# Linear attention: where a unit's score matmuls stand in TensorE's hand-written order

## Chip, cores, metric

One core of a Trainium2 chip runs the whole program in one launch. The metric is the device time of that launch in microseconds; 14 runs of the kernel before gave a median of 2377.67 us, from 2363.53 to 2383.84.

## What is computed

The program is a stack of four layers on `x` of shape (4, 1024, 128) in float32. Each layer is an attention-like part and a feed-forward part, each with a residual and a layer norm. Only the third layer's attention and feed-forward part, and how they interleave, matter here. The attention is a causal linear attention with 16 heads of 64, written in the reference as a scan over time:

```python
Qp, Kp = relu(x @ Wq + bq), relu(x @ Wk + bk)      # V = x @ Wv + bv
Qc, Qs = Qp * cos(a_t), Qp * sin(a_t)              # a_t = pi * t / (2 T)
Kc, Ks = Kp * cos(a_t), Kp * sin(a_t)
S_cos += Kc_t V_t^T ; S_sin += Ks_t V_t^T ; z_cos += Kc_t ; z_sin += Ks_t
out_t = (Qc_t S_cos + Qs_t S_sin) / max(Qc_t z_cos + Qs_t z_sin, 1e-6)
y = out @ Wo + bo
```

The feed-forward part is a mixture of 8 experts: a softmax router picks two per row, and each row's result is the weighted sum of two gated MLPs (128 to 2 x 256 to 128).

## The kernel before, in words

**Units.** The attention (`l2_attn`, L920) cuts the time axis of each of the four sequences into four quarters of 256 rows, and each quarter into eight pairs of heads: 128 units. In a unit the 256 rows are two chunks (c) of 128. Within a chunk the kernel uses the product form: scores of all keys with all queries, multiplied by a fixed matrix (`c_near`: the cosine of the distance, zero above the diagonal). What lies before a chunk comes from running sums of keys with values, carried from chunk to chunk.

**The steps of a unit.** The letters in the list are only for reading:

- `l2_project` (L1045): TensorE makes the queries and keys of the unit (tile pqk, a bank called pj); ScalarE applies relu and writes r_q and r_k; GpSimd multiplies r_q with the cosines and sines (qt).
- `l2_keys` (L1065): two TensorE transposes of r_k into the bank kp; ScalarE writes them out four times scaled (kN). In the last quarter of a sequence only one chunk's keys are needed.
- `l2_scores` (L1106): eight matmuls, 16 instructions in the trace since each float32 matmul takes two passes, of 64 rows by 64 columns, into the banks pa0 and pa1. VectorE multiplies each of the two with `c_near` and writes the tile a (L1119), which holds the scores for the next step.
- `l2_before` (L1138): queries qt with the carried sums st, into the bank po.
- `l2_within` (L1154): a with the values cv, on top of it in po.
- `l2_sums` (L1082): kN with the values, 128 rows by 64 columns, into the bank kp (pst); VectorE adds the carried sums and writes the new ones, st (L1098 to L1103; one or two instructions).
- `l2_out` (L1164): VectorE divides: dn (L1171), a reciprocal, co (L1173).

**The order on TensorE.** TensorE's order in this stage is the order in which the loop at L966 issues; `manual_schedule` at L965 says so. Iteration t holds work of three units: keys of unit t+1, projection of unit t+2, scores of t+1, then before and within of unit t, the sums of t+1, and l2_out of t. All other engines have an order made by a scheduler. Between the sums and the next iteration's key transposes stands extra work that only some iterations have: values of the next quarter (pv, VectorE evacuates them as cv), output transposes (pt, ScalarE copies them as coT), output projections (pr), the normalisation of four chunks and its transposes, the router and the dispatch of the experts. A list `side` of generators advances one step per iteration.

**The expert tiles.** Once a sequence's rows are dispatched, `early(moe)` at L988 advances the mixture of experts by one tile of 128 rows per iteration: every fourth time the transposes of four row tiles (pt<-xg), then the hidden matmuls of one tile (`l2_hidden`, L1474: eight instructions), then the output of the tile two before (`l2_expert_out`, L1498: py, four instructions). ScalarE and VectorE make tanh, sg and mh out of the hidden matmuls; ScalarE copies py to ys.

**Shared banks.** Three PSUM banks are shared by slices, which is written in three lines:

```python
for t in (("pa0", "m0"), ("pa1", "m1"), ("kp", "mo")):
    v = two.tile([P, 512], F32, name="_".join(t))
    self.psq.update({t[0]: (v, 0), t[1]: (v, 3 * P if t[0] == "kp" else 2 * P)})
```

So pa0 takes the left half of a bank for the scores and m0 the right half for the experts' hidden matmuls; likewise pa1 and m1; and kp holds key transposes and pst on the left, and mo, the expert output py, on the right. There is one buffer of each. The trace calls these tiles pa_m and kp_mo.

Of the kernel before, what the change touches and what calls it, by code (L numbers as in the profile page):

```python
# [58 lines left out]
class Net:  # L59
# [42 lines left out]
    def load(self, name, shape, pool=None, tag=None, eng=None):  # L102
        pool = pool or self.const
        t = pool.tile(shape, F32, name=f"sb_{name}", tag=tag or f"sb_{name}")
        src = self.io[name]
        (eng or self.nc.sync).dma_start(out=t, in_=src)
        return t
# [812 lines left out]
    def l2_attn(self, load, dispatch, moe, first):  # L920

        nc, tc = self.nc, self.tc
        NQ = 2
        with ExitStack() as ctx:
            wp = ctx.enter_context(tc.tile_pool(name="cos", bufs=2))
            self.c2["wp"] = wp  # L930
            quarters = [
                dict(b=b, q=q, c0=q * NQ, x=self.xT[b][:, q * NQ * P : (q + 1) * NQ * P])
                for b in range(B)
                for q in range(NC // NQ)
            ]
            units = [dict(Q=Q, hp=hp) for Q in quarters for hp in range(NP2)]
            self.psq = {}
            for t, n in dict(pj=2, po=1).items():
                self.psq[t] = ctx.enter_context(
                    tc.tile_pool(name=f"ps_{t}", bufs=n, space=bass.MemoryType.PSUM)  # L940
                )

            two = ctx.enter_context(
                tc.tile_pool(name="ps_two", bufs=1, space=bass.MemoryType.PSUM)
# [4 lines that stand above are left out]
            v = two.tile([P, 512], F32, name="pr_sx")  # L949
            self.psq.update(pr=(v, 0), sx=(v, 2 * P))  # L950
            self.mtags = dict(t="pj", h=("m0", "m1"), o="mo")
            self.l2_tiles(quarters[0], None)
            for f in self.l2_values(quarters[0]):
                pass
            n = len(units)
            side, begin = [], None

            def early(moe):

                if "done" not in self.m2["st"][1]:  # L960
                    for k in range(1):
                        next(moe)


            ctx.enter_context(tc.manual_schedule(engines={mybir.EngineType.PE}))  # L965
            for t in range(-2, n + 4):  # L966
                if t == 0:
                    load()
                if 0 <= t + 1 < n:
                    u = units[t + 1]  # L970
                    if u["hp"] == 0:
                        i = (t + 1) // NP2
                        if i + 1 < len(quarters):
                            nxt = quarters[i + 1]
                            self.l2_tiles(nxt, quarters[i])
                            side.append(self.l2_values(nxt))
                    self.l2_keys(u)
                if 0 <= t + 2 < n:
                    self.l2_project(units[t + 2])
                if 0 <= t + 1 < n:  # L980
                    self.l2_scores(units[t + 1])
                if 0 <= t < n:
                    self.l2_before(units[t])
                    self.l2_within(units[t])
                if 0 <= t + 1 < n:
                    self.l2_sums(units[t + 1])
                if "put" in self.m2["st"][0] if t > 0 else False:
                    early(moe)  # L988
                    if "done" in self.m2["st"][0]:

                        if begin is None:
                            begin = self.l3_prepare(self.l3_early(first))
                        next(begin, None)
                if 0 <= t < n:
                    self.l2_out(units[t])
                    if t % 4 == 3:
                        Q = units[t]["Q"]
                        g = self.l2_project_out(Q, t % NP2 // 4)
                        if t % NP2 == NP2 - 1 and Q["c0"] + NQ == NC:
                            g = chain(g, dispatch(Q["b"]))  # L1000
                        side.append(g)
                for g in side[:]:
                    if next(g, self) is self:
                        side.remove(g)
            for g in (begin, *side):
                for f in g:
                    if f == "put":
                        self.m2["rest"] = g
                        break
# [1193 lines left out]
```

## Time and profile before

| what | number |
|---|---|
| median of 14 runs | 2377.67 us (2363.53 to 2383.84) |
| the profiled execution | 2381.47 us, span 2379.7 us |
| granted TensorE clock, mean over the span | 0.907 |
| first and last score multiplication a (L1119) | 643.3 and 1369.3 us |
| hidden matmuls of experts in the attention's banks | 360 instructions, 988.7 to 1384.6 us |

The attention is the stretch from about 641 to 1375 us. After it follows the last layer, a state-space layer and another mixture of experts, with the remaining expert tiles in between.

In the views, PE is TensorE, PEld its weight loads, DVE VectorE, ACT ScalarE, POOL GpSimd. A row of the timeline gives start, duration, engine, line, operation, output tile <- input tiles and shape; in square brackets stands the engine's idle time before it and what ended it. Neighbouring instructions of one kind are merged into one row (x16), so a matmul row's start is the start of its group and its duration ends with the last, modelled, end. Matmuls overlap: the time a group costs is read from its start to the start of the next group. A row of the waits reads "engine, tile, line <- engine, tile, line that ended the wait: us in total, times, longest". A row of the table of stages gives the stretch, its length, then busy time and instruction count of PE, PEld, DVE, ACT and POOL, the granted clock, the DMA share and GB/s.

### The profile page before, as it was taken

The page shows a single profiled execution, that of the slowest core. Times are in us where ns is not written, and L with a number is a line of the kernel's source. Part 1 is how long each engine was busy: PE and PEld are TensorE (multiplying, and loading weights), DVE is VectorE, ACT ScalarE, POOL GpSimd, SP SyncE. Part 2 cuts the span into 40 slices and gives each one's busy share as a digit, 9 for nine tenths or more (in the row PEclk, how much of TensorE's full clock was granted, in tenths as well). Part 3 has the DMA queues.
Part 4 walks back from the last instruction along what each step waited for, and adds up shares of the span by engine and source line. Part 5 has one row for each costly group of instructions (what it writes and reads, how often), then busy time and mean ns, then how long its engine had stood idle before and what let it go on. Part 6 is the DMA issues. An engine that isn't in the chain of part 4 may idle for free. (4 is left out here: it accounts for less than half of the span.)

```text
span 2379.7 us, 46470 instructions
## 1 busy us (share of the span) xinstructions
PE 2035.2 (86%) x17858; PEld 1425.4 (60%) x17858; DVE 1349.5 (57%) x3661; ACT 1206.0 (51%) x2619; POOL 1025.3 (43%) x813
## 2 busy tenths in 40 slices
PE   6667979879999999999979856778898989799988
PEld 3455655444477777787767654345565556465666
DVE  6457733433355554654545536776767777676421
ACT  6543433332244444454446536565758776667443
POOL 5001220000123234134143328988887998678400
PEclk9757969979999999999989978979999999899999
DMA  3000110005000010021222046555775766575411
GB/s 103 0 18 18 31 35 1 18 13 164 1 3 3 2 36 23 24 86 36 78 70 82 16 157 189 165 161 173 207 208 140 202 172 178 165 196 157 118 58 49
DMA packets 138702, 211.63 MB, mean 89 GB/s; under 512 B 18613, under 2 KB 75952, under 8 KB 138096
## 3 DMA queue, kind: packets, MB, share of 16 engines
q1 hardware_dynamic: 126192, 173.87, 23.8%
q0 software_dynamic: 12288, 34.79, 6.9%
q8 instruction: 141, 2.31, 0.4%
q14 instruction: 81, 0.66, 0.1%
HBM read 160.29 MB, written 23.16 MB: 77 GB/s over the span
## 5 line engine op out<-in xcount | busy, mean ns | idle before, releaser
L1061 POOL TENSOR_TENSOR qt<-r_q,sb_c_turn 128x256 f32<-128x256 f32 (+1 forms) x256 | 164.3, 663 | 460.7 <-ACT r_q L1053 455.1
L1861 POOL TENSOR_TENSOR hc<-db,cn 128x1024 f32<-128x1024 f32 x128 | 311.7, 2460 | 72.9 <-PE pys L127 24.4
L1845 POOL TENSOR_TENSOR db<-ud,bn 128x1024 f32<-128x1024 f32 x112 | 283.7, 2590 | 32.6 <-DVE ud L1809 16.8
L127 PEld LDWEIGHTS py<-wh,hh 128*128 128x128 f32 x2048 | 253.8, 197 | 72.8 <-issue 37.0
L127 PE MATMUL ph<-xT,wh 128*128 128x512 f32 x512 | 264.1, 633 | 24.1 <-ACT hh L1973 5.2
L127 PE MATMUL py<-wh,hh 128*128 128x128 f32 x2048 | 260.0, 281 | 17.5 <-ACT hh L1973 14.1
L1973 ACT ACTIVATE hh<-ph,sb_cols 128x512 f32<-128x512 f32 x256 | 171.8, 682 | 136.3 <-PE ph L127 109.5
L1119 DVE TENSOR_TENSOR a<-pa_m,sb_c_near 128x256 f32<-128x256 f32 x256 | 96.5, 419 | 215.1 <-PE pa_m L127 215.1
L1076 ACT ACTIVATE kN<-kp_mo,sb_c_trig 128x128 f32<-128x128 f32 x448 | 130.1, 372 | 132.1 <-PE kp_mo L131 119.3
L1849 ACT ACTIVATE da<-dl,aneg 128x512 f32<-128x512 f32 x224 | 153.4, 689 | 75.6 <-DVE db L1850 67.8
L127 PE MATMUL pys<-hc,sb_c_ident 128*128 128x512 f32 x320 | 163.0, 635 | 9.8 <-DMA hc<-hc 6.4
L1850 DVE TENSOR_TENSOR_SCAN db<-da,carry,db 128x512 f32<-128x512 f32 x128 | 157.2, 1266 | 11.7 <-ACT da L1849 7.0
L127 PEld LDWEIGHTS ph<-xT,wh 128*128 128x128 f32 x512 | 91.6, 200 | 114.4 <-issue 56.0
L1850 DVE TENSOR_TENSOR_SCAN db<-da,db 128x512 f32<-128x512 f32 x128 | 149.7, 1206 | 8.9 <-ACT da L1849 5.7
L1989 DVE SCALAR_TENSOR_TENSOR h_acc<-py,gt,h_acc 128x128 f32<-128x128 f32 x256 | 71.6, 342 | 138.2 <-PE py L127 138.2
L127 PE MATMUL pqk<-xT,wE 128*128 128x256 f32 x512 | 139.5, 396 | 7.9 <-ACT coT L1195 4.2
L729 POOL DMA_INDIRECT orows<-o,ix x20 | 18.9, 945 | 203.3 <-DVE o L727 169.1
L127 PEld LDWEIGHTS pys<-hc,sb_c_ident 128*128 128x128 f32 x320 | 61.6, 205 | 73.3 <-issue 59.0
L127 PEld LDWEIGHTS pqk<-xT,wE 128*128 128x128 f32 x512 | 90.6, 197 | 22.4 <-DVE cv L1038 8.1
L1195 ACT COPY coT<-pt 128x512 f32<-128x512 f32 x64 | 37.5, 586 | 125.5 <-PE pt L131 125.5
L131 PE MATMUL pt<-sb_c_ident,xN 128*128 128x128 f32 x224 | 54.1, 344 | 51.9 <-ACT xN L174 33.9
L127 PE MATMUL po<-ht,wD 128*128 128x512 f32 x192 | 93.7, 595 | 0.0
(450 smaller groups left out, 4403.8 us busy)
## 6 DMA issues: line engine op xcount, KB each, us to landing
wx<-in_wF SPq DMA_DIRECT2D x92, 384.0 KB
bn<-rows SPq DMA_DIRECT2D x128, 256.0 KB
cn<-rows SPq DMA_DIRECT2D x128, 256.0 KB
wh<-in_wH SPq DMA_DIRECT2D x64, 512.0 KB
hc<-hc POOLq DMA_DIRECT2D x48, 512.0 KB
xrows<-zero SPq DMA_DIRECT2D x4, 1472.0 KB
xg<-xrows SPq DMA_DIRECT2D x20, 256.0 KB
yrows<-ys SPq DMA_DIRECT2D x20, 256.0 KB
```

The lines of the kernel that those rows point to most:

```text
L127: return self.nc.tensor.matmul(out=out, lhsT=lhsT, rhs=rhs, start=start, stop=stop)
L131: self.nc.tensor.transpose(out, in_, self.ident[0:n, 0:n])
L1061: nc.gpsimd.tensor_mul(u["qt"][:, m, a:], u["q"][:, a:], c2["turn"][:, m, o + a : o + 2 * P])
L1076: self.nc.scalar.activation(u["kN"][:, c, m, :], pk[:, c, :], AF.Copy, scale=trig[:, k, m : m + 1])
L1119: nc.vector.tensor_mul(u["a"][:, i, :, :], pa[i], self.c2["near"][:, None, :].to_broadcast([P, 2, P]),)
L1195: nc.scalar.copy(oT, pt)
L1845: nc.gpsimd.tensor_mul(db, ud, bc[0])
L1849: nc.scalar.activation(da, dl[:, ec, :], AF.Exp, scale=aneg[:, j : j + 1])
L1850: nc.vector.tensor_tensor_scan(db[:, ec, :], da, db[:, ec, :], carry[:, ec, n : n + 1] if h else 0.0, ALU.mult, ALU.add,)
L1861: nc.gpsimd.tensor_mul(hc, db, bc[1])
L1973: nc.scalar.activation(ht, ph, AF.Relu, bias=self.col("h_b1", i=e * NK + k))
L1989: nc.vector.scalar_tensor_tensor(acc[:, c, :], py[:, c, :], gt[:, c, e : e + 1], acc[:, c, :], ALU.mult, ALU.add,)
```

## The change

The scores of unit t+1 are issued behind the sums of unit t+1 and no longer behind the projection of unit t+2. In an iteration TensorE's order was keys, projection, scores, before, within, sums; it is now keys, projection, before, within, sums, scores, and then the expert tile and the side work as they were. Scores of a unit are still made one iteration ahead of the within step that uses them.

```diff
                     self.l2_keys(u)
                 if 0 <= t + 2 < n:
                     self.l2_project(units[t + 2])
-                if 0 <= t + 1 < n:
-                    self.l2_scores(units[t + 1])
                 if 0 <= t < n:
                     self.l2_before(units[t])
                     self.l2_within(units[t])
                 if 0 <= t + 1 < n:
                     self.l2_sums(units[t + 1])
+                    self.l2_scores(units[t + 1])
                 if "put" in self.m2["st"][0] if t > 0 else False:
                     early(moe)
```

## The prediction

> **What bounds the kernel now.** I read the page's first two parts, then the table of stages (busy time of each engine in three stretches of the linear attention), then TensorE's waits in those stretches, then the timeline of single units. The profiled execution took 2381.47 us around a span of 2379.7; the median of the 14 runs is 2377.67, so what I work out in this trace is added to the median.
>
> ```profile
> span 2379.7 us, 46470 instructions
> PE 2035.2 (86%) x17858; PEld 1425.4 (60%) x17858; DVE 1349.5 (57%) x3661; ACT 1206.0 (51%) x2619; POOL 1025.3 (43%) x813
> ```
>
> ```profile
> 640.00:985.00 345.00, 323.21 (x6037) 259.03 (x6035) 185.98 (x623) 149.71 (x437) 110.95 (x182) 0.98 0.04 12
> 985.00:1305.00 320.00, 291.67 (x4668) 243.67 (x4668) 173.63 (x637) 157.19 (x466) 104.55 (x150) 0.95 0.23 68
> 1305.00:1375.00 70.00, 59.14 (x1049) 47.78 (x1047) 38.40 (x116) 37.38 (x85) 22.07 (x28) 0.93 0.11 31
> ```
>
> In each row the second number is the length and the third TensorE's (PE's) busy time: 94%, 91% and 84%. The attention runs from 641 to 1375 us and TensorE bounds it; VectorE (DVE) is about half busy. What TensorE waits for there is short:
>
> ```profile
> PE kp_mo L131 <- DVE st L1103: 14.6, 14, 2.7
> PE kp_mo L127 <- DVE st L1103: 10.1, 5, 2.2
> ```
>
> Both rows are one kind of wait: the bank that is named kp in its left columns and mo in its right columns is written again only after VectorE has read the key-value sums (pst) out of it. In the first row the next unit's key transposes wait, in the second the expert output py. That one writes the mo columns, which the sums never touch, and waits all the same.
>
> A unit with no extra work, whose end shows the first wait:
>
> ```profile
> 710.15 0.67 PE L127 MATMUL pa_m<-r_q,r_k 64*64 64x128 f32 x16
> ...
> 710.63 0.65 PE L1128 MATMUL po<-st,qt 64*64 64x65 f32 x32
> ...
> 711.21 0.69 PE L1128 MATMUL po<-cv,a 128*64 128x65 f32 x16
> ...
> 711.73 0.64 PE L127 MATMUL kp_mo<-cv,kN 128*64 128x65 f32 x16
> ...
> 712.69 0.28 DVE L1100 TENSOR_TENSOR st<-kp_mo,st 128x130 f32<-128x130 f32 x1
> 713.01 0.29 DVE L1103 TENSOR_TENSOR st<-kp_mo,st 128x130 f32<-128x130 f32 x1
> ...
> 713.45 0.41 PE L131 MATMUL kp_mo<-sb_c_ident,r_k 128*128 128x128 f32 x2 [1.08 <-DVE st L1103]
> ```
>
> Read the starts: scores 710.15, before 710.63, within 711.21, sums 711.73; VectorE ends its second st at 713.30 and the transposes start 0.15 later, 2.24 after within. VectorE needs that long because dn, the reciprocal, co and two st stand one behind another once within is done. And a unit that also carries an expert tile:
>
> ```profile
> 1037.53 0.69 PE L1128 MATMUL po<-cv,a 128*64 128x65 f32 x16
> ...
> 1038.62 1.16 PE L127 MATMUL pa_m<-xgT,wx 128*128 128x128 f32 x8
> ...
> 1039.33 0.29 DVE L1103 TENSOR_TENSOR st<-kp_mo,st 128x130 f32<-128x130 f32 x1
> ...
> 1039.68 0.71 PE L127 MATMUL kp_mo<-wx,mh 128*128 128x128 f32 x4
> ```
>
> The expert's hidden matmuls start right behind the sums, 1.09 after within, and write the m0 and m1 columns of the two banks whose pa0 and pa1 columns take the scores.
>
> **The change, part by part.** No instruction is added or removed; 16 score matmuls of each of 128 units move, and with them the two multiplications a. No DMA and no GpSimd work moves.
>
> *(1) The scores leave their place before before.* They take 0.48 us there (710.15 to 710.63). So within, the sums, and VectorE's dn to st come 0.48 earlier after the transposes. The keys kN must then be ready 0.48 earlier for the sums: in most units ScalarE ends the last kN 0.7 to 1.9 us ahead of the sums, so this costs nothing. (In one unit with little slack, at 1283, up to 0.4 would show.)
>
> *(2) The scores come behind the sums.* They cost 0.48 again, and one change of array shape more than before. Today a unit changes from 128x128 to 64x64 (into the scores), to 128x64 (into within) and back to 128x128: three. Afterwards: into before, into within, into the scores, and back: four. Price of one from the rows: before's 32 instructions run at 0.058 per four, which is 0.46, but within starts 0.58 after them, 0.11 more; the projection's four run at 0.215 each and the scores start 0.10 later than that pace. I take 0.10. Bounds: nothing, as from within to the sums, which share a shape, and 0.15. The Trainium skill, "TensorEngine Tiling (Array Packing)", Key Properties, says that a change of tiling mode drains the engine, which speaks against the new place and agrees with these spacings; without such a cost the 73 units of (3) that pay it would keep 7 us.
>
> *(3) The wait of the transposes shrinks.* The moved scores, about 0.59 with their changes of shape, lie in it. Where the wait is longer than that, a unit gains the whole 0.48; where there is none it loses 0.10; in between it loses 0.10 less the wait. Over the 88 units without an expert tile, from the start of each unit's groups: 11 with 0.6 to 1.16 us of wait (the unit without extra work; a first output transpose that waits for co) gain 0.48, in sum -5.3; 12 with waits of 0.19 to 0.59 give -3.2; 8 with 0.16 behind pr give -0.4; four, where a normalisation or the state-space work on VectorE or ScalarE ends last, give 0, since that chain starts from r_q and r_k and not from the scores; the other 53 lose 0.10, +5.3. Sum: **-3.6 us**.
>
> *(4) The multiplication a is now fresh when the expert's matmuls come.* In the built program's order VectorE has dn, reciprocal, co, st, st, a, a in every unit. The expert's first hidden matmul waits for an a on pa0 and its third for the a on pa1, in both programs; but so far these were a of scores issued two groups of matmuls earlier, long done, and now they are the a of the scores just in front. The price: st ends at within + 2.09 (1039.62 - 1037.53); an a takes 0.415 and two in a row 0.75, so one behind st adds 0.34; the release takes 0.15 as above. The hidden matmuls start at within + 2.58 in place of 1.09: 1.49 later, and with (1)'s 0.48 back, **+1.01 per unit**. The second a ends 0.34 after the first, while the first four hidden matmuls take 0.45, so it adds nothing. Behind them stand the expert output, values, output projection and the next transposes on TensorE, all of which shift; tanh, sg and mh shift too, but their tile is used two units later. (2)'s switch and the scores themselves vanish in this wait.
>
> The page has 45 tiles' hidden matmuls (360 instructions, eight each); 5 come after the last scores, 40 inside. 21 plain ones: 21 x 1.01 = 21.2. Ten have row transposes xg ahead (hidden at within + 1.58 today): 1.00 less 0.48, 5.2. Four are in a last quarter with one st: there a waits for the scores instead (they end about within + 1.5), +0.8 each, 3.2. Five are units with a normalisation, where py waits for a late st today; afterwards the hidden matmuls start 0.49 behind that st (0.34 and 0.15) and py 0.89 later (eight at the 0.11 that four in 0.45 make), where it was 0.15: 1.23 each, 6.2; the 0.48 isn't regained, since the chain to that st starts from r_q and r_k. Sum: **+35.8 us**.
>
> The Trainium skill, "PSUM — Partial Sum Buffer", section on bank collisions, tells authors to guard by bank and quadrant, not by address; by that rule the wait in (4) is needed, while by addresses (4) would fall away, these units would lose about 0.10 each, and the total would be near zero. The row of py that waits for st is the trace's own case of the former.
>
> *After the attention* the order on ScalarE and VectorE differs in places (two table loads of 1.28 fewer on ScalarE). I cost it at 0, within 5 us either way. The state-space stage follows on the same engines, so the delay passes on.
>
> **Sum:** -3.6 + 35.8 = +32, so 2381.5 + 32 = 2413.5 in the terms of the profiled run, **2410 us** against the median.
>
> **The rivals.**
>
> *The wait (4) is not exposed* (6%): if both a were done by the time the hidden matmuls are reached, about 1.7 after within, they would start at once. Nothing in VectorE's own speed speaks for it: a stands behind st in the order, and st alone ends at within + 2.09. Then the 40 units lose 0.10 each, +4.0, and the sum is 2378: no change.
>
> *Shape changes cost nothing and the wait shrinks* (6%): with (4) not exposed and a switch price of 0 in place of 0.10, the 113 units that pay it (53, 12 and 8 without an expert tile, the 40 with one) keep 11.3, and 2367 is left: faster, by over 0.3% once a switch costs under 0.04. The spacing from within to the sums speaks for it, the other two and part (4) against.
>
> *The new waits also lower the clock or meet a second bound* (15%): TensorE would stand idle some 1 us in each of 40 units; the table's granted clock falls from 0.98 to 0.95 already where idle is greatest. If the expert stretch fell to 0.92, its 292 busy us would grow by about 9: 2420. Against it: between 645 and 750 waits of 1.1 us recur and the clock stands at 1.00.
>
> *Waits partly taken back* (8%): where the transposes today wait 0.52 for the copy of py, or where DMA or a normalisation ends last, a shift of 1.01 may overlap; half of (4): 2392.
>
> **How the numbers follow.** The forecast, 65%, 2400 to 2420 by (2)'s bounds and the 5 us of the tail. Range with the neighbours 2390 to 2424. A measurement of this kernel can tell about 0.3%, 7 us, from no change. Faster 6%, within 0.3% 6%, slower 88%.
>
> **What would show it.** TensorE's waits must show hidden matmuls (pa_m<-xgT,wx) held by DVE a for 0.7 to 1.1 us some 40 times; transposes held by st much less (14.6 us to about 8); units without extra work 4.0 us apart and not 4.5; units with plain expert tile 6.8 where they were 5.8. If hidden matmuls do not wait, (4) is wrong and with it the sign; if the spacing from the sums to the scores is 0.05, (2) is.

## The result, and the profile after

The changed kernel takes **2403.6 us** (median of 13 runs, 2396.1 to 2415.7), the kernel before 2377.05 in the same comparison (62 runs): a ratio of 1.0117 [1.0102, 1.0132], 26.6 us more. The forecast was 2410, within 2390 to 2424.

The profiled execution was shorter than the 13 timed ones (2394.0 us around its span); a second profile of the same program has a span of 2414.7. The page of the first:

```profile
span 2392.2 us, 46443 instructions
...
PE 2029.8 (85%) x17858; PEld 1415.7 (59%) x17858; DVE 1336.4 (56%) x3661; ACT 1201.8 (50%) x2617; POOL 1023.5 (43%) x813
```

TensorE does the same 17858 instructions in no more busy time (2029.8 us for 2035.2); what is new is time between them. The table of stages, with borders shifted so that each stretch holds the same work as the row of before:

```profile
635.00:980.00 345.00, 329.68 (x6036) 258.09 (x6035) 179.64 (x623) 149.05 (x437) 110.41 (x182) 0.99 0.04 12
980.00:1328.00 348.00, 299.54 (x4667) 243.75 (x4666) 168.80 (x636) 157.86 (x466) 104.14 (x150) 0.95 0.22 62
1328.00:1395.00 67.00, 56.76 (x1051) 44.86 (x1049) 38.01 (x117) 36.92 (x86) 22.02 (x28) 1.00 0.11 33
```

The first stretch, without expert tiles, is as long as before (345). The second, which has nearly all of them, grew from 320 to 348 at the same granted clock of 0.95. The third lost 3. So the loss is in the stretch with the expert tiles, and on the mean it isn't the clock. What TensorE waits for between 640 and 1405 us:

```profile
PE pa_m L127 <- DVE a L1118: 35.2, 33, 3.5
...
PE kp_mo L131 <- DVE st L1102: 7.3, 11, 1.5
```

The first row is new: matmuls that write the pa/m banks, held by the multiplication a (L1118 is L1119 of before). The second is the wait that the change shortens: it had 14.6 us. The row of py held by st (10.1 us) is gone. Who waits for a, from the view of that line:

```profile
who waited for it (us, times):
  PEld pa_m L127: 45.8, 40
  PE pa_m L127: 35.2, 33
  ACT L1489: 9.1, 4
```

Weight loads in front of hidden matmuls wait 40 times, as many as there are expert tiles inside the attention. A unit without extra work, in the timeline:

```profile
704.85 0.70 PE L1127 MATMUL po<-st,qt 64*64 64x65 f32 x32
...
705.48 0.69 PE L1127 MATMUL po<-cv,a 128*64 128x65 f32 x16
...
706.00 0.64 PE L127 MATMUL kp_mo<-cv,kN 128*64 128x65 f32 x16
...
706.56 0.67 PE L127 MATMUL pa_m<-r_q,r_k 64*64 64x128 f32 x16
...
707.28 0.29 DVE L1102 TENSOR_TENSOR st<-kp_mo,st 128x130 f32<-128x130 f32 x1
...
707.72 0.41 PE L131 MATMUL kp_mo<-sb_c_ident,r_k 128*128 128x128 f32 x2 [0.49 <-DVE st L1102]
```

The scores (706.56) lie where TensorE stood idle. The transposes still start 2.24 after within, but within comes 0.46 earlier, and the unit takes 4.05 us in place of 4.51. That is the gain. A plain unit with an expert tile shows the price:

```profile
1037.94 0.69 PE L1127 MATMUL po<-cv,a 128*64 128x65 f32 x16
...
1038.45 0.64 PE L127 MATMUL kp_mo<-cv,kN 128*64 128x65 f32 x16
...
1039.02 0.67 PE L127 MATMUL pa_m<-r_q,r_k 64*64 64x128 f32 x16
...
1039.73 0.29 DVE L1102 TENSOR_TENSOR st<-kp_mo,st 128x130 f32<-128x130 f32 x1
1039.94 0.74 DVE L1118 TENSOR_TENSOR a<-pa_m,sb_c_near 128x256 f32<-128x256 f32 x2
1040.04 0.98 POOL L1382 DMA_INDIRECT xrows<-xN,di  x1 [0.16 <-issue]
1040.41 0.30 PEld L127 LDWEIGHTS pa_m<-xgT,wx 128*128 128x128 f32 x2 [0.97 <-DVE a L1118]
1040.41 0.38 PE L127 MATMUL pa_m<-xgT,wx 128*128 128x128 f32 x1 [0.73 <-DVE a L1118]
```

The scores are issued by 1039.6, and then TensorE stands until VectorE, which has dn, the reciprocal, co and two st ahead of it, is through with the first a. The hidden matmuls start 2.47 after within, where it was 1.09.

### The profile page after: what moved, and what is told of

The parts are those of the page before. It is cut to its first block, busy times and chain, and to the rows that moved or that the text cites. A ratio compares the mean times of both kernels' runs of the same rounds, so it can differ in the third digit from the quotient of the medians.

```text
span 2392.2 us, 46443 instructions
## 1 busy us (share of the span) xinstructions
PE 2029.8 (85%) x17858; PEld 1415.7 (59%) x17858; DVE 1336.4 (56%) x3661; ACT 1201.8 (50%) x2617; POOL 1023.5 (43%) x813
## 4 chain that ended last, share of the span: by engine, by line
PE 41%; DVE 14%; ACT 11%; issue 4%; DMA 2%; POOL 1%; SPq 0%; DVEq 0%; ACTq 0%; POOLq 0%
PE py L127 7%; PE ph L127 7%; PE po L1127 6%; DVE db L1849 5%; PE pqk L127 4%; PE pa_m L127 4%; PE pr_sx L1197 3%; PE pys L127 2%; PE pv L127 2%; PE kp_mo L127 2%; ACT da L1848 1%; PE pt L131 1%; ACT hh L1972 1%; DMA wx<-in_wF 1%; PE kp_mo L131 1%
## 5 line engine op out<-in xcount | busy, mean ns | idle before, releaser
L1860 POOL TENSOR_TENSOR hc<-db,cn 128x1024 f32<-128x1024 f32 x128 | 329.7, 2605 | 57.3 <-DVE db L1849 19.6
L1844 POOL TENSOR_TENSOR db<-ud,bn 128x1024 f32<-128x1024 f32 x112 | 300.3, 2726 | 36.4 <-DVE ud L1808 22.6
L127 PE MATMUL ph<-xT,wh 128*128 128x512 f32 x512 | 254.2, 615 | 22.4 <-ACT hh L1972 7.2
L1170 DVE TENSOR_SCALAR dn<-po 128x4 f32<-128x4 f32 x128 | 20.5, 160 | 252.4 <-PE po L1127 252.3
L1118 DVE TENSOR_TENSOR a<-pa_m,sb_c_near 128x256 f32<-128x256 f32 x256 | 95.3, 414 | 0.5 <-PE pa_m L127 0.5
```

What stands on the lines that cost most here:

```text
L127: return self.nc.tensor.matmul(out=out, lhsT=lhsT, rhs=rhs, start=start, stop=stop)
L1118: nc.vector.tensor_mul(u["a"][:, i, :, :], pa[i], self.c2["near"][:, None, :].to_broadcast([P, 2, P]),)
L1844: nc.gpsimd.tensor_mul(db, ud, bc[0])
L1860: nc.gpsimd.tensor_mul(hc, db, bc[1])
```

## The experiments

The theory: the loss is the wait of the hidden matmuls for the fresh a, and it exists because their results share banks with the scores. The rivals: the late place costs by itself (array shapes, later values and projections), or the time behind the attention changes. "Attention" is, in each profile, the time from the first key transposes to the last co; "behind" is from there to the end.

| kernel | ratio to before [interval] | attention, us | behind, us |
|---|---|---|---|
| before (two profiles) | 1 | 732.6, 732.5 | 1005.8, 1002.7 |
| changed (two) | 1.0117 [1.0102, 1.0132] | 757.5, 763.2 | 998.5, 1012.8 |
| late_where_no_tile (two) | 1.0023 [1.0007, 1.0040] | 727.6, 728.3 | 1013.0, 1009.9 |
| late_where_tile | 1.0124 [1.0100, 1.0148] | 763.5 | 1007.9 |
| after_hidden_pj (two) | 0.9990 [0.9975, 1.0004]; 0.9986 [0.9969, 1.0003] | 724.8, 725.9 | 1015.9, 1015.8 |
| before_hidden_pj | 0.9993 [0.9972, 1.0013] | 734.4 | 1004.4 |
| scores_behind_side | 1.0060 [1.0039, 1.0081] | 748.2 | 1000.3 |
| late_where_it_pays | 0.9936 [0.9915, 0.9957] | 715.0 | 1016.4 |

**The new place only in units without, or only in units with, an expert tile.** TILES are the 40 iterations that carry a tile; the second kernel has the two conditions swapped.

```diff
+TILES = {*range(69, 84), *range(93, 116), *range(125, 127)}
...
+                tile = t in TILES
+                if 0 <= t + 1 < n and tile:
+                    self.l2_scores(units[t + 1])
                 if 0 <= t < n:
                     self.l2_before(units[t])
...
                     self.l2_sums(units[t + 1])
+                if 0 <= t + 1 < n and not (tile):
                     self.l2_scores(units[t + 1])
```

> Scores behind the sums in the 88 iterations without an expert tile, in the old place in the 40 with one. Theory (the cost is the hidden matmuls' wait for the fresh a; without a tile the move only shortens the transposes' wait): 4 to 8 us faster than before, 2370 to 2374 us, and no row of hidden matmuls waiting for a. Rival (the late place itself costs, by its extra change of array shape or by an altered order on the other engines): 5 us slower than before or more.

> The other half alone: scores behind the sums only in the 40 iterations with an expert tile. Theory: all of the loss and a little more than it, 28 to 36 us over before, some 2405 to 2413; each plain tile unit about 0.8 us longer. Rival (the late place itself costs): about a third of the loss, +9 us, since 40 of 128 units have it.

With the new place only beside tiles: 2405.6, 28 us over before; the whole loss, as expected. Without them: 2382.9, 5.6 us over before, where 4 to 8 less were expected: a miss. Its attention did get 4 to 5 us shorter. What was lost lies behind it: 1013.0 and 1009.9 us in place of 1005.8 and 1002.7. That stretch, which the edit doesn't touch, was to change by no more than 5 us in the prediction; what goes along with it is told below, under the second profiles.

**The hidden sums in a bank of their own.** They go to a buffer of pj, which the projections and the output transposes use, in the changed kernel and in the one before.

```diff
-            self.mtags = dict(t="pj", h=("m0", "m1"), o="mo")
+            self.mtags = dict(t="pj", h=("pj",), o="mo")
```

> The changed kernel with the experts' hidden matmuls in one of the two pj banks, so that they share no bank with the scores; their four matmuls then share one bank, and tanh, sg and mh are one instruction each over both halves. Theory: hidden matmuls start 0.2 us behind the scores, no wait for a, and this kernel is within 7 us of its partner with the old order of scores (before_hidden_pj). Rival (the loss is not the shared bank): still 20 us or more over its partner.

> The kernel before with the hidden matmuls in a pj bank: the partner of the run above. Both theories: within 10 us of the kernel before either way; a pj bank is busier, but tanh, sg and mh are fewer instructions. It only sets the level to compare with.

This decides it. With the order of the change left as it is, the loss is gone: 2375.0 and, in a second comparison, 2379.9 beside 2381.2. In the kernel before the same edit moves nothing that could be measured. The same unit as above, in the timeline of after_hidden_pj (the hidden sums are called ph here):

```profile
1036.92 0.69 PE L1127 MATMUL po<-cv,a 128*64 128x65 f32 x16
...
1038.01 0.67 PE L127 MATMUL pa_m<-r_q,r_k 64*64 64x128 f32 x16
...
1038.61 1.16 PE L127 MATMUL ph<-xgT,wx 128*128 128x128 f32 x8
1038.73 0.29 DVE L1102 TENSOR_TENSOR st<-kp_mo,st 128x130 f32<-128x130 f32 x1
...
1038.94 0.75 DVE L1118 TENSOR_TENSOR a<-pa_m,sb_c_near 128x256 f32<-128x256 f32 x2
```

The hidden matmuls start right behind the scores, 1.69 after within, and a runs beside them. In this kernel's view of the line of a, the list of those who waited for it is empty.

**The scores at the very end of a unit.** Behind the expert tile and the side work.

```diff
                     self.l2_sums(units[t + 1])
-                    self.l2_scores(units[t + 1])
                 if "put" in self.m2["st"][0] if t > 0 else False:
                     early(moe)
...
                     if next(g, self) is self:
                         side.remove(g)
+                if 0 <= t + 1 < n:
+                    self.l2_scores(units[t + 1])
```

> The scores of the next unit come at the very end of a unit in TensorE's order: behind the sums, the expert's tile and the other extra work. By the theory (the loss is the hidden matmuls that wait for the multiplications a of the scores just in front of them) the hidden matmuls then start right behind the sums again, about 1.1 us after within, and no hidden matmul waits for a. The other way round the scores now wait for the readers of the hidden sums, about 0 to 0.5 us in the units where the expert output is the last extra work. Expected: 2374 to 2388 us, no more than 0.5% from the kernel before. By the rival (the loss comes from the late place itself: shape changes, or key transposes and the next unit's values that come late) it stays at 2395 us or above, as in the changed kernel.

2391.3 beside 2375.1: 0.6% where at most 0.5% (2388) was expected, a miss, and 4 us below the rival's 2395. The mechanism held: hidden matmuls start 0.567 behind the start of the sums, as in the kernel before. TensorE's waits have the other way round, and little of it, and no row with a:

```profile
PE pa_m L127 <- DVE mh L1494: 1.6, 4, 0.4
```

What remains is not that wait. The stretches with tiles are 3.1 and 2.7 us longer than in before (11.0 and 16.9 in the changed kernel), but the first stretch, which has none, is 8.7 longer. In most units the scores now stand between groups of 128 by 128 on both sides, with one more change of array shape than in the changed kernel, and most units grow step by step: with values and projection 5.18 in before, 5.34 in the changed kernel, 5.49 here; with projection and transposes 4.78, 4.94, 5.07. This isn't all of it: units with values, projection and transposes are up to 0.25 shorter than in before, and no run took the shape change away alone.

**The new place where it pays.** Hidden sums in pj, and the scores early in 63 iterations (EARLY) in which, between before_hidden_pj and after_hidden_pj, the late place had made a unit 0.10 to 0.55 us longer.

```diff
-            self.mtags = dict(t="pj", h=("m0", "m1"), o="mo")
+            self.mtags = dict(t="pj", h=("pj",), o="mo")
...
+                early_t = t in EARLY
+                if 0 <= t + 1 < n and early_t:
+                    self.l2_scores(units[t + 1])
...
-                    self.l2_scores(units[t + 1])
+                if 0 <= t + 1 < n and not early_t:
+                    self.l2_scores(units[t + 1])
```

> The hidden sums in their own bank, and the new place of the scores only in the 64 iterations in which it shortened a unit by more than the added change of array shape costs or left it equal; in the 63 others (mostly units with values or an output projection behind the sums, each 0.16 us longer in the late place) the scores stay ahead of before. By the theory each of those 63 units gets its 0.16 us or more back, 63 units with 11.3 us in the two profiles with the hidden sums moved: the attention, 724.8 us from the first key transposes to the last co with the scores late everywhere and 732.6 in the kernel before, should take 714 to 718 us. The whole: 2375 less 7 to 11 is 2364 to 2368, a ratio of 0.995 to 0.997. By the rival (the gains hang on the neighbouring units and on the order that VectorE and ScalarE are given, and what the attention gains is lost behind it) 2372 or more.

> The changed kernel with the hidden sums in their own bank, once more. Attention from the first key transposes to the last co 724.8 us as in the first profile, within 1 us. The stretch behind the last co was 1015.9 us, the longest of all profiles: if it varies from execution to execution it comes out several us away, if it belongs to the program within 2 us. Time 2371 to 2378.

2367.2 beside 2381.2: 14 us faster than before, a little more than expected, and the attention took 715.0 us, within the 714 to 718 named. It beats both kernels. Beside after_hidden_pj, run on the same chip, it is 12.8 us faster. The stretch behind the attention stayed at 1016.4 in the one profile, an execution of 2375.5 us, 8 above the median.

**Second profiles, for the time behind the attention.**

> The kernel with the new place only where a unit carries no expert tile, once more for a second profile. Its attention was 5 us shorter than before's and the stretch behind the attention 7 us longer. If that stretch differs from execution to execution, it should come out different here by several us from 1013.0 us (last co to the end); if the program itself makes it longer, within about 2 us of 1013.0.

> The kernel before, a second profile: the stretch behind the last co took 1005.8 us in the first. If it varies from execution to execution, it comes out several us away; if it belongs to the program, within about 2 us.

> The changed kernel, a second profile: the attention should be the same within 1 us (last co at about 1393.8 us, hidden matmuls held by a as before); the stretch behind the last co took 998.5 us in the first. Since the first profiled execution was 9.6 us under the median of the timed ones, I expect a longer stretch here, about 1003 to 1012 us, if the spread lies behind the attention.

The attention repeats within 1.1 us for each of these programs except the changed kernel, where it differs by 5.7: jumps of 0.5 to 2.1 in four units where a run of expert tiles begins or ends. At these places the second profile's granted clock is 0.5 for 3.4 or 6.8 us longer than the first's.

Behind the attention, two profiles of a program are 0.1 to 3.1 us apart, and 14 in the changed kernel. From program to program the stretch goes from 998.5 to 1016.4. late_where_it_pays and after_hidden_pj have the same order of instructions on all engines there, and the same 1016; before_hidden_pj has another order and 1004. But late_where_tile has the changed kernel's order, and these three profiles spread from 998.5 to 1012.8, so the order doesn't settle it. The granted clock goes along with the time: in this stretch it is 0.92 in before, before_hidden_pj, late_where_tile and the changed kernel (998.5 to 1012.8 us), 0.91 in late_where_no_tile (1013.0, 1009.9) and 0.90 in after_hidden_pj and late_where_it_pays (1015.8 to 1016.4). TensorE is busy there for 843.1 and 839.4 us in before and for 853.6 to 856.7 in the last two, with as many instructions. scores_behind_side (1000.3 us at 0.91) does not fit. No run held the order or the clock alone: whether the order sets the clock, or something else does, stays open.

## Why the prediction was right

**The sign and its cause, step (4).** Held: 40 waits for a were forecast and 40 found, and taking the shared bank away takes the loss away. VectorE's order, which the prediction gives as the same in every unit, is dn, reciprocal, co, st, st, a, a in 87 of the 128; in the others an st stands ahead of co. That these sums share only a bank with the scores, and no column, is what the Trainium skill's "PSUM — Partial Sum Buffer" tells authors to guard (bank collisions); the program has that wait, and no run here shows what would happen without it.

**Its size.** A plain unit with a tile was forecast to lose 1.01 and lost **0.79** (5.46 to 6.24, 5.83 to 6.62, 6.69 to 7.48). The terms, from medians of group starts: the hidden matmuls came 0.10 earlier than costed, at within + 2.48, since the release took 0.05 (in the unit shown the first a ends at 1040.36) and not 0.15; before grew by 0.05 (a shape change at its entry); and hidden and output groups are 0.17 shorter, which the prediction had not seen: in the kernel before py waited for st in every such unit, and behind a it no longer does. 1.01 - 0.10 + 0.05 - 0.17 = 0.79. Units with row transposes lost 0.57 (0.52 forecast), last-quarter units 0.76 (0.8). Of the five units with a normalisation (1.23 forecast) iterations 82, 98, 112 and 114 lost 2.25, 2.97, 1.96 and 2.53, and 106 came out 1.19 shorter; some neighbours gave part of it back. In those four TensorE waited 2.4 to 3.2 us for a, and next to the start of the hidden matmuls the granted clock went to 0.5 for 3.4 us, so that they took 1.35 to 1.87 us up to py and not 1.00; in the kernel before this comes in one of the four, at the end of iteration 82. In late_where_tile, with the same late scores, iterations 82 and 114 have no such stretch and lost 0.64 and 0.88. So part of what they lost is the clock, which the prediction had only in a rival. All stretches with tiles, up to the last co: +11.0, +16.9 and +1.2, together **+29.1** in the first profile and +34.8 in the second, for a forecast of +35.8.

**The change of array shape, step (2).** Costed at 0.10 with 0.15 as the upper bound; measured **0.16**, outside it. From group start to group start the scores take 0.597 behind the sums, where they took 0.488, and before takes 0.626 (32 instructions) where it took 0.575. The prediction counted one change more and took the price of one. But two spacings grew, the way out of the scores into 128 by 128 by 0.11 and the way into before by 0.05.

**The shorter wait, step (3).** Units without extra work came out at 4.05 (4.0 forecast), the wait for st at 7.3 us (about 8). The sum of units without tiles is -4.3, for -3.6; but that is two misses that cancel. In the 79 units ahead of the state-space work 17 units gained 8.0, 43 lost 0.16 each, 6.9 in all, and the other 19 lost 1.4: +0.3. The last stretch, costed at nothing, gave -4.6, 3.6 of it in one unit. There VectorE had dn, the reciprocal and co between three multiplications of the state-space layer, and TensorE's output transposes waited 3.5 us for co; in the changed kernel co stands ahead of them.

**The rivals.** "Not exposed" and "shape changes cost nothing" fall by the 40 waits and the 0.16. The clock did not fall as a whole: 0.95 before and after in the stretch with tiles, and 0.92 in both behind the attention (the table of before has its lowest clock, 0.93, in the third row, where TensorE is least busy, and not 0.95 as the prediction reads it). It fell in single units, the four above. "Waits partly taken back" is what happened to py, 0.17 of the 1.01, and not to half of it.

**The sum.** Attention +24.9 and +30.7 in the two profiles, +27.8 on the mean, and behind it 1005.7 on the mean for 1004.3: together +29, for +32 forecast and +26.6 measured. That the stretch behind comes out near the 0 it was costed at is luck: the two profiles, 998.5 and 1012.8, lie on either side, further off than the 5 us allowed. The two profiles of the changed kernel differ by 22.5 us in span; 14.3 of it lie behind the attention and 5.7 in it.

## What to carry to other kernels

When a group of matmuls is moved into an idle gap, look for what is issued behind it and writes to the same bank: a wait that was long satisfied becomes fresh, and the reader that releases it may stand last in another engine's queue. Take the shared bank apart first, and then decide the place unit by unit: here that turned 1.2% more time into 0.6% less. Measure also the part of the program that the edit should not touch, with its granted clock: here it moved by as much as the gain.

## What had not been expected of the hardware

A group of 64 by 64 matmuls pays for the change of array shape on both sides, by unequal amounts: 0.05 us more ahead of before when it comes from the projection and not from the scores, 0.11 from the scores into 128 by 128. Units in which the 16 score instructions stand between two 128 by 128 groups, which is one change more again, were another 0.13 to 0.15 us longer, in units of 5 us. The Trainium skill's "TensorEngine Tiling (Array Packing)", Key Properties, says that a change of tiling mode drains TensorE, which agrees with these spacings. A matmul released by VectorE started 0.05 us after the end of the a that it waited for, and the transposes 0.15 after st. Waits of 2.4 to 3.2 us were followed in four units by 3.4 us at a granted clock of 0.5; the longest, 3.5 us in iteration 125, was not in the first profile of the changed kernel, and in the second the clock was at 0.5 for 6.8 us around its end.
